# One more step of lead for projections and norms in a hand-scheduled transformer kernel

## The chip, the core and the metric

The kernel runs on one core of a Trainium2 chip. The metric is the device time in microseconds (us) of one execution, and the figure given is the median over runs. TensorE is called PE in the profile, VectorE DVE, ScalarE ACT, GpSimd POOL, SyncE SP. PEld is PE's loading of weights.

## The reference, cut to what matters

The input is 2048 tokens of 128 features. Three modules follow each other: a stack of six local-attention layers, a linear-attention block, and the same stack once more. One layer of the stack is what the change is about:

```python
def attn_layer(x, Wqkv, qs, ksc, Wo):            # 16 heads of 64, windows of 32 tokens
    q, k, v = jnp.split(x @ Wqkv, 3, -1)         # ... split into heads
    q = l2norm(q) * qs
    k = l2norm(k) * ksc
    q = q * cos * scale + rotate_half(q) * sin * scale
    k = k * cos * inv + rotate_half(k) * sin * inv
    out = local_attention(q, k, v)               # each window sees itself and the one before
    return out.transpose(0, 2, 1, 3).reshape(b, n, INNER) @ Wo

def ffn_layer(x, g, bln, W1, b1, W2, b2):
    xn = (x - mu) / jnp.sqrt(var + 1e-05) * g + bln
    a, gate = jnp.split(xn @ W1 + b1, 2, -1)
    return a * jax.nn.gelu(gate, approximate=False) @ W2 + b2

for i in range(DEPTH):                           # DEPTH = 6
    x = attn_layer(shift_tokens(x), ...) + x
    x = ffn_layer(shift_tokens(x), ...) + x
```

The token shift moves half of the features by one token.

## The kernel before

**Tiles and stages.** Features lie on the 128 partitions, tokens along the free axis. A layer is cut into 8 chunks of 256 tokens (`AC`), and the attention of a chunk into 4 steps (`STEPS`): two halves of 128 tokens by two halves of 8 heads. The feed-forward works on blocks of 512 tokens, so one block goes with two chunks, that is with eight steps.

**Order.** Nothing here is left to a planner. The inner function `at(step, pos, fn, ...)` of `ffn_module` (L552) enters a call into a plan under a step and a position in it; at the end the calls are made step by step, in a step by position, inside `manual_schedule` (L599). Each engine carries out its own instructions in that order, and waits where an input or a buffer is not ready. A module has 6 x 8 x 4 = 192 steps, and some more at both ends. `t0` is the first attention step of a chunk.

**The work of one chunk, in the order of its data:**

- `tables` (L187) multiplies the rotation tables by a layer's scales, on POOL, four instructions for q and four for k.
- `project` (L203), four calls g = 0 to 3: eight matmuls p (L218, each instruction of the source runs as two) give a quarter of q and of k in two banks. DVE multiplies each with the tables into `prod` (L224), POOL adds the two halves into `abq` or `abk` (L230), and ACT squares each bank into `sq` (L236). The order of issue is rotation of q, square of k, square of q, rotation of k.
- `square_sums` (L247), two calls: matmuls ss (L254) add the squares up by head into the one bank of `ps_ss`.
- `norms_a` (L310): a maximum on DVE (L314), then Ln, Exp and Square on ACT (L315, L316, L318), which give a first estimate of the inverse norms in `rn`. `norms_b` (L321): two DVE instructions (L325, L326) that refine it.
- `scale_keys` (L342), two calls: four matmul instructions r (L347) spread the norms of the keys over the partitions, into two banks; two DVE multiplies (L353) scale `abk`; then `gather` (L293) issues eight DMAs on SP's queue that lay out the keys in `hk`. Queries are gathered in the same way into `hq`, straight after projection, and their norms go through `query_norms` (L328) into `rq`.
- `values_proj` (L261) and `values_windows` (L276): v by matmul pv (L271), a copy on ACT (L272), and three DMAs on SP into `ve` and `vo`.
- `earlier_keys` (L358): the last window of the chunk before, rotated by matmul pk (L367).
- In the chunk's own steps: `similarities` (L372) with a mask matmul (L383), 32 matmul instructions (L391) and a maximum and a product on DVE (L402, L403, the statistics `st`); `exponentials` (L407), eight on ACT (L417); a step later `normalised` (L424), a reciprocal on DVE and a multiply on POOL; another step later `transposed` (L435), with matmuls te (L443) and copies eT on DVE (L444), and `values` (L446), with matmuls av (L458) and a copy oT on ACT (L464); then `output` (L466), matmuls y (L471) and additions on DVE (L475).
- `feed_forward` (L479) is a generator of which eight pieces are placed at odd steps mostly: mean and squares (`lnsq`), variance, `rstd`, its spreading `rb`, three times a pair of matmuls pf (L513) with a GELU gate on ACT (L518) and a product h on DVE (L522), then yf (L530). Around each gate ACT loads another table set and then the former one (L516, L521).

**Banks.** All matmul results but similarities and square sums come from one pool of five PSUM banks, `small` (L182). A new tile takes the bank that came free longest ago, and PE waits when its readers are not done. `rn` has one buffer, `sq` four, `prod` two, `abq` two and `abk` three.

**Where things stand before.** In numbers of steps modulo 4, with the position in brackets: projection (20) in all steps, its g = 0 in step 1; square sums (45) in steps 2 and 0; `norms_a` (2) and `norms_b` (33) in step 1; `scale_keys` (58) in step 1 and (45) in step 2; values (50) in all steps; gates (57) in steps 3, 1 and 3 of eight.

Of the kernel before, what the change touches and what calls it, by code (L numbers as in the profile page):

```python
# [40 lines left out]
def kernel(ctx: ExitStack, tc: tile.TileContext, a: dict, out: bass.AP):  # L41
# [84 lines left out]
    def ffn_module(m, last):  # L126
        with ExitStack() as st:
# [424 lines left out]
            def at(step, pos, fn, *args):  # L552
                plan.setdefault(step, []).append((pos, len(plan[step]) if step in plan else 0, fn, args))
# [5 lines left out]
            for l in range(DEPTH):  # L559
                for c in range(NAC):  # L560

                    t0 = per * l + STEPS * c
                    if c == 0:
                        at(t0 - 10, 46, tables, l, 0)
                        at(t0 - 8, 46, tables, l, 1)
                    for g in range(4):
                        at(t0 - 7 + g, 20, project, l, c, g)
                        at(t0 - 2 + g, 50, values_proj, l, c, g)
                    for g2 in range(2):
                        at(t0 - 6 + 2 * g2, 45, square_sums, l, c, g2)  # L570
                    for t in range(2):
                        at(t0 - 1 + 2 * t, 62, values_windows, l, c, t)
                    at(t0 - 5, 30, gather, l, c, "q", 0)
                    at(t0 - 3, 1, gather, l, c, "q", 1)
                    at(t0 - 3, 2, norms_a, l, c)
                    at(t0 - 3, 33, norms_b, l, c)
                    at(t0 - 3, 58, scale_keys, l, c, 0)
                    at(t0 - 2, 45, scale_keys, l, c, 1)
                    at(t0 - 2, 46, query_norms, l, c)
                    at(t0 - 1, 45, earlier_keys, l, c)  # L580
                    for s in range(STEPS):
                        at(t0 + s, 25, similarities, l, c, s)
                        at(t0 + s, 30, exponentials, l, c, s, 0)
                        at(t0 + s, 51, exponentials, l, c, s, 1)
                        at(t0 + s + 1, 3, normalised, l, c, s)
                        at(t0 + s + 2, 40, transposed, l, c, s, 0)
                        at(t0 + s + 2, 41, transposed, l, c, s, 1)
                        at(t0 + s + 2, 60, values, l, c, s)
                    for t in range(2):
                        at(t0 + 4 + 2 * t, 55, output, l, c, t)  # L590
                for f in range(NCH):
                    gen = feed_forward(l, f)
                    t0 = per * l + 8 * f
                    for step, pos in (
                        (11, 57), (12, 57), (13, 4), (13, 57),
                        (15, 57), (17, 57), (19, 57), (21, 57),
                    ):
                        at(t0 + step, pos, more, gen)
# [112 lines left out]
    def no_earlier():  # L711

        nc.gpsimd.memset(xa[64:P, 0:1], 0.0)

    ffn_module(0, False)
    linear_module()
    no_earlier()
    ffn_module(1, True)


# [103 lines left out]
```

## Time and profile before

| What | Value |
|---|---|
| Median of 3 runs | 4289.59 us (4288.85 to 4295.82) |
| The profiled execution | 4295.45 us |
| Its span, first to last instruction | 4293.6 us |
| Mean granted TensorE clock | 0.959 |
| PE, PEld | 92%, 64% of the span |
| DVE, ACT, POOL | 63%, 66%, 39% |
| Linear-attention block and norms between the stacks | about 2050 to 2240 us, PE busy 135.84 of 190 us |
| Eight key or query DMAs | some 5 us of SP's queue, 2.1 us to landing for each |

The busy share of an engine is an average over the whole span. A wait is named by the instruction that waits and the one that released it, with the total in us, the number of times and the longest. A line number (L218) is one of the listing above; te, pv, y, av, r, p, pf are the names of PSUM tiles. In a timeline the columns are start, duration, engine, line, operation, tiles written and read, count, and in brackets the idle time before it with its releaser. Busy time of PE is modelled from the starts of its matmuls.

### The profile page before, as it was taken

To read this page: it belongs to the slowest core of one execution; us is meant where nothing else is said; L and a number is where in the kernel's file an instruction comes from. 1 tells how busy PE (TensorE), PEld (TensorE's weight loads), DVE (VectorE), ACT (ScalarE), POOL (GpSimd) and SP (SyncE) were. 2 spreads that over 40 slices of the span, in tenths; PEclk is the share of its full clock that TensorE was granted. 3 is DMA by queue.
4 is the path that set the end of the run, shared out by engine and by line. 5 is a ranking of instruction groups with operands and counts; after the bars stand their busy time and mean duration, and the time that the engine had idled before them with its cause. 6 is when DMAs were issued, how large, how long until landed. Compare 5 with 4: busy or idle time off the path is not lost.

```text
span 4293.6 us, 110203 instructions
## 1 busy us (share of the span) xinstructions
PE 3947.0 (92%) x41968; PEld 2744.5 (64%) x41968; DVE 2719.7 (63%) x5222; ACT 2846.8 (66%) x8784; POOL 1672.7 (39%) x1355
## 2 busy tenths in 40 slices
PE   7899999999999999999777899999999999999998
PEld 4666666666666666666445666666666666666665
DVE  4666666666676666665426566666666666766664
ACT  4676777767667676677225676767667676677766
POOL 4343444344344334332014344343343443443331
PEclk8999999999999999999788999999999999999998
DMA  3343433433334334342003343433434334343331
GB/s 105 86 107 89 101 100 94 103 94 101 97 92 112 93 95 110 87 102 68 8 25 91 85 109 89 104 98 96 101 95 107 93 96 106 87 109 97 91 99 49
DMA packets 323975, 393.67 MB, mean 92 GB/s; under 512 B 61052, under 2 KB 274808, under 8 KB 323448
## 3 DMA queue, kind: packets, MB, share of 16 engines
q1 hardware_dynamic: 323448, 386.61, 35.7%
q8 instruction: 334, 5.47, 0.5%
q14 instruction: 193, 1.58, 0.1%
HBM read 34.58 MB, written 1.05 MB: 8 GB/s over the span
## 4 chain that ended last, share of the span: by engine, by line
PE 23%; ACT 16%; DVE 7%; issue 2%; SPq 1%; DMA 1%; POOL 1%; ACTq 0%; DVEq 0%; POOLq 0%
ACT e L417 8%; PE p L218 5%; DVE prod L224 3%; PE y L471 2%; PE te L443 2%; ACT L516 2%; PE pv L271 2%; PE av L458 2%; PE sim L391 2%; PE ss L254 2%; SPq L305 1%; ACT v L272 1%; DVE sim L402 1%; ACT gate L518 1%; PE yf L530 1%
## 5 line engine op out<-in xcount | busy, mean ns | idle before, releaser
L417 ACT ACTIVATE e<-sim,st,rq 128x96 f32<-128x96 f32 x3072 | 1291.8, 440 | 570.9 <-DVE st L403 509.5
L429 POOL TENSOR_TENSOR e<-e,st 128x768 f32<-128x768 f32 x384 | 564.4, 1470 | 1869.1 <-DVE st L427 1540.3
L224 DVE TENSOR_TENSOR prod<-p,tab 128x1024 f32<-128x1024 f32 x768 | 918.6, 1211 | 235.5 <-ACT sq L236 129.4
L218 PE MATMUL p<-xa,wqk 128*128 128x256 f32 x3072 | 845.0, 420 | 120.4 <-ACT gate L518 115.4
L218 PEld LDWEIGHTS p<-xa,wqk 128*128 128x128 f32 x3072 | 592.0, 204 | 246.6 <-ACT gate L518 138.1
L236 ACT ACTIVATE sq<-p 128x512 f32<-128x512 f32 x768 | 435.6, 599 | 355.6 <-PE p L218 240.0
L417 ACT ACTIVATION_READ_ACCUMULATOR e<-sim,st,rq 128x1 f32 x3072 | 653.9, 213 | 0.0
L230 POOL TENSOR_TENSOR abq<-prod 128x512 f32<-128x512 f32 x384 | 489.0, 1273 | 188.2 <-DVE prod L224 144.4
L230 POOL TENSOR_TENSOR abk<-prod 128x512 f32<-128x512 f32 x384 | 485.7, 1265 | 72.5 <-DVE prod L224 63.7
L444 DVE COPY eT<-te 96x512 f32<-96x512 f32 x768 | 489.8, 677 | 3.6 <-PE te L443 3.6
L522 DVE SCALAR_TENSOR_TENSOR h<-pf,lvec,gate 128x512 f32<-128x512 f32 x144 | 107.9, 749 | 571.1 <-ACT gate L518 553.1
L471 PEld LDWEIGHTS y<-oT,wo 128*128 128x128 f32 x3072 | 374.4, 192 | 95.1 <-issue 49.5
L402 DVE TENSOR_REDUCE sim<-sim 128x4 f32<-128x384 f32 x768 | 426.5, 555 | 9.0 <-PE sim L391 8.8
L443 PE MATMUL te<-sq_consts,e 128*96 128x128 f32 x3072 | 424.1, 279 | 2.5 <-ACT gate L518 0.8
L271 PE MATMUL pv<-wv,xa 128*128 128x512 f32 x768 | 415.4, 623 | 10.6 <-DVE rstd L499 8.4
L458 PE MATMUL av<-eT,ve 96*64 96x64 f32 x6144 | 406.9, 229 | 4.6 <-DVE eT L444 4.5
L458 PEld LDWEIGHTS av<-eT,ve 96*64 96x64 f32 x6144 | 318.3, 138 | 132.5 <-issue 50.5
L272 ACT COPY v<-pv 128x512 f32<-128x512 f32 x384 | 227.6, 593 | 255.3 <-DMA ve<-v 171.1
L458 PE MATMUL av<-eT,vo 96*64 96x64 f32 x6144 | 385.8, 223 | 0.0
L471 PE MATMUL y<-oT,wo 128*128 128x128 f32 x3072 | 376.4, 276 | 4.5 <-ACT gate L518 3.0
L391 PEld LDWEIGHTS sim<-hk,hq 64*64 64x64 f32 x12288 | 279.1, 136 | 151.7 <-issue 136.4
L443 PEld LDWEIGHTS te<-sq_consts,e 128*96 128x96 f32 x3072 | 317.6, 127 | 59.5 <-DVE h L522 11.8
(141 smaller groups left out, 4954.9 us busy)
## 6 DMA issues: line engine op xcount, KB each, us to landing
hq<-abq SPq DMA_DIRECT2D x1536, 64.0 KB, 2.1
hk<-abk SPq DMA_DIRECT2D x1536, 64.0 KB, 2.1
vo<-v SPq DMA_DIRECT2D x192, 384.0 KB, 4.3
ve<-v SPq DMA_DIRECT2D x192, 256.0 KB, 3.5
ve<-v SPq DMA_DIRECT2D x180, 128.0 KB, 2.3
wqk<-in_Wqk SPq DMA_DIRECT2D x48, 256.0 KB, 3.6
wv<-in_Wv SPq DMA_DIRECT2D x24, 256.0 KB, 2.8
wo<-in_Wo SPq DMA_DIRECT2D x12, 512.0 KB, 5.0
```

What stands on the lines that cost most here:

```text
L218: nc.tensor.matmul(both[s][:, u, :], wqk[g][:, 2 * s + u, :], xs, start=True, stop=True)
L224: nc.vector.tensor_tensor(prod, both[s].unsqueeze(2).to_broadcast([P, 2, 2, AC]), tabs[l, s].rearrange("p (u v) t -> p u v t", u=2), ALU.mult,
L230: nc.gpsimd.tensor_tensor(d["qk"[s], g // 2][:, :, g % 2, :], prod[:, 0], prod[:, 1], ALU.add)
L236: nc.scalar.activation(sq, both[s], AF.Square)
L271: nc.tensor.matmul(ps, xa[:, ti * P : (ti + 1) * P], wv[j], start=True, stop=True)
L402: nc.vector.tensor_reduce(peaks[par], sims[par], AX.X, ALU.max, negate=True)
L417: nc.scalar.activation(e[:, par, i, :], d["sims", step][par][:, i, :], AF.Exp, bias=st8[:, 0, par, i : i + 1], scale=rq[:, par, i : i + 1] ...
L429: nc.gpsimd.tensor_tensor(ef, ef, st8[:, 1].rearrange("p r i -> p (r i)").unsqueeze(2).to_broadcast([P, 8, SK]), ALU.mult,)
L443: nc.tensor.transpose(te3[0:SK, i, :], d["e", step][:, par, i, :], ident)
L444: nc.vector.tensor_copy(d["eT", step][:, 4 * par : 4 * par + 4, :], te3[0:SK])
L458: nc.tensor.matmul(av3[64 * par : 64 * par + 64, i, SQ * s : SQ * s + SQ], d["vs", t][s][:, h * DH : (h + 1) * DH], d["eT", step][:, 4 * p ...
L471: nc.tensor.matmul(y[:, 0:P], wo[:, i, :], d["oT", t][:, i, :], start=(i == 0), stop=(i == 7))
```

## The change

Only the plan's numbers change. Each call does what it did.

- `tables` and `project` run one step earlier; so do `square_sums`, which also go from position 45 to 61, behind the products with v.
- `norms_a`, `norms_b` and the second gather of queries run one step earlier, at the positions that they had.
- `scale_keys` stay in their steps and go from positions 58 and 45 to 27, directly behind the similarities (25) and ahead of the first exponentials (30).

```diff
                     if c == 0:
-                        at(t0 - 10, 46, tables, l, 0)
-                        at(t0 - 8, 46, tables, l, 1)
+                        at(t0 - 11, 46, tables, l, 0)
+                        at(t0 - 9, 46, tables, l, 1)
                     for g in range(4):
-                        at(t0 - 7 + g, 20, project, l, c, g)
+                        at(t0 - 8 + g, 20, project, l, c, g)
                         at(t0 - 2 + g, 50, values_proj, l, c, g)
                     for g2 in range(2):
-                        at(t0 - 6 + 2 * g2, 45, square_sums, l, c, g2)
+                        at(t0 - 7 + 2 * g2, 61, square_sums, l, c, g2)
                     for t in range(2):
                         at(t0 - 1 + 2 * t, 62, values_windows, l, c, t)
                     at(t0 - 5, 30, gather, l, c, "q", 0)
-                    at(t0 - 3, 1, gather, l, c, "q", 1)
-                    at(t0 - 3, 2, norms_a, l, c)
-                    at(t0 - 3, 33, norms_b, l, c)
-                    at(t0 - 3, 58, scale_keys, l, c, 0)
-                    at(t0 - 2, 45, scale_keys, l, c, 1)
+                    at(t0 - 4, 1, gather, l, c, "q", 1)
+                    at(t0 - 4, 2, norms_a, l, c)
+                    at(t0 - 4, 33, norms_b, l, c)
+                    at(t0 - 3, 27, scale_keys, l, c, 0)
+                    at(t0 - 2, 27, scale_keys, l, c, 1)
                     at(t0 - 2, 46, query_norms, l, c)
```

After it the square sums stand in steps 1 and 3 modulo 4, the norms in step 0, and projection g = 0 in step 0.

## The prediction, on record before the result

> **What bounds the kernel now.** I read the page first (busy shares), then TensorE's waits, then the timelines of PE, ACT and DVE over one cycle of eight steps, then the granted clock in small windows.
>
> ```profile
> PE 3947.0 (92%) x41968; PEld 2744.5 (64%) x41968; DVE 2719.7 (63%) x5222; ACT 2846.8 (66%) x8784; POOL 1672.7 (39%) x1355
> ```
>
> PE is nearly always busy, so an edit pays only through PE's gaps. Its waits (total us, times, longest):
>
> ```profile
> PE p L218 <- ACT gate L518: 115.4, 84, 1.9
> PE ss L254 <- ACT sq L236: 54.9, 50, 4.2
> PE r L347 <- DVE rn L326: 33.9, 10, 5.5
> ```
>
> The schedule repeats every eight steps (two chunks, one feed-forward block); I number a step by its index modulo 8. Starts of the projection matmuls (p) give one clean cycle, 601.27 to 683.19 us, 81.92 us: steps 4, 5, 6, 7, 0, 1, 2, 3 last 11.20, 10.12, 10.18, 8.20, 10.69, 10.70, 11.80 and 9.03. The first wait in the list has two members per cycle, 0.87 us in step 4 and 1.88 us at the start of step 2 (44 x 1.88 + 40 x 0.87 = 117.5, against 115.4). The square sums wait 0.91 us in step 0; r waits 0.30 in step 1. Together 3.96 us of stall. The 1.88 us one has a second cost:
>
> ```profile
> 660.45:662.36 1.91, 0.03 (x3) 1.00 0.00 0
> 662.36:665.70 3.34, 3.34 (x10) 0.60 0.03 8
> ```
>
> Columns: stretch, length, PE busy, granted clock. Behind the stall the clock falls to 0.60 here (0.50 elsewhere) and eight p matmuls take 3.16 us, not 1.99; with mask and similarities this cycle lost 1.67 us. From 2715.20 to 4117.43 us there are 17 cycles of 82.48 us on average, so the mean loss is 1.67 + 0.56 = 2.2 us.
>
> The steps with a GELU gate are 7, 1 and 3. Here ACT after step 3's exponentials, then DVE and PE in step 4 (which starts at 601.27):
>
> ```profile
> 601.23 1.28 ACT L516 ACT_TABLE_LOAD   x1
> 602.53 0.68 ACT L518 ACTIVATE gate<-pf,lvec 85x512 f32<-85x512 f32 x1
> 603.23 1.28 ACT L521 ACT_TABLE_LOAD   x1
> 604.62 0.63 ACT L89 ACTIVATE lnsq<-xc 128x512 f32<-128x512 f32 x1
> 605.16 0.57 ACT L464 COPY oT<-av 128x512 f32<-128x512 f32 x1
> 605.62 1.09 ACT L236 ACTIVATE sq<-p 128x512 f32<-128x512 f32 x2
> ```
> ```profile
> 606.32 1.22 DVE L224 TENSOR_TENSOR prod<-p,tab 128x1024 f32<-128x1024 f32 x1 [0.54 <-ACT sq L236]
> ...
> 608.80 1.27 DVE L444 COPY eT<-te 96x512 f32<-96x512 f32 x2
> ```
> ```profile
> 603.27 1.13 PE L218 MATMUL p<-xa,wqk 128*128 128x256 f32 x4 [0.87 <-ACT gate L518]
> ...
> 606.48 1.34 PE L254 MATMUL ss<-sq,sel 128*32 128x256 f32 x16
> ...
> 611.38 0.33 PE L458 MATMUL av<-eT,ve 96*64 96x64 f32 x4
> ```
>
> The reader is to see a chain: gate and its two table loads hold ACT until 604.5, the squares start 4.35 us into step 4 (2.03 in a step without gate before it), the second rotation waits for a square, the eT copies end 8.8 us in, and PE reaches the products with v (av) only at 10.1. PE's own work is just long enough to hide the gate.
>
> [...] the trace shows DVE's rotation waiting 0.54 us for ACT's square of the same bank. [...]
>
> **The change, part by part.**
>
> *Spread of key norms (scale_keys) to position 27.* The 1.88 us exists because step 1 hands out banks in the order pf, pf, r, r, av, and with five banks, passed on in the order in which they come free, the next p takes the one that the gate reads. With r ahead of the transposes, p takes the banks of te and pv, free long before; the gate's two go to r, 3.1 us into step 2, when gate and h are over. Gone: 1.88 us, the 0.30, and the clock loss behind it. What is late next: the tile 5 allocations behind r. r's readers are two DVE multiplies (0.60 us apart) that start after the reductions, 5.2 us into a step, so r's banks come free at 5.9 and 6.5. In step 2 pv takes the first; PE is there at 1.83 + 0.42 + 0.82 + 0.63 + 0.95 + 0.55 = 5.2 (p, mask, similarities, r, te, nt). Stall 0.7 in step 6, and 1.2 in step 2, where the gate makes DVE some 0.4 late. In steps 1 and 5 pf and yf take it: PE at 5.45, stalls 0.5 and 0.6. Sum 3.0 us of new stall. eT copies are 1.25 us later (7.7), av comes at 7.8 or later: hidden. The price could lie below nothing only if DVE ran ahead of today's rows; upper end 4.5.
>
> *Square sums to position 61.* ss (1.00 to 1.28 us) moves from even to odd steps. Its 0.91 us wait goes, and so does its place in front of av. Steps 3 and 7, 1 and 5 get 1.0 us longer; 4, 0, 2 and 6 shorter by 1.28, 1.61, 1.0 and 1.0. In step 4 the 0.87 us goes too: ss now lies between the gate's matmuls and p.
>
> *Norms one step earlier: the costly part.* norms_a (ACT Ln, Exp, Square: 652.53 to 653.69 in the timeline, 1.16 us; DVE maximum 0.43) and norms_b (DVE, 0.79) were in steps 1 and 5, behind a step with no gate. Now they are in steps 0 and 4, always right behind a gate of step 7 or 3, in the chain above and ahead of squares and eT copies. Step 4: squares 13.38 us after step 3's start become 14.54; second rotation 15.24; statistics 17.7; norms_b 18.5; eT 19.8. PE starts step 4 at 9.03 + 1.0 and is at av 8.0 later, 18.05. Step 4 then ends at 19.8 + 1.09 = 20.9 after step 3's start (20.23 now). Step 0, without lnsq: squares 13.99 after step 7's start, eT 19.25, PE at av 16.05, end 20.35 (18.89 now). PE's idle time there is 3.2 us in step 0 (about 1 of it ahead of y, whose bank waits for a square) and 2.0 in step 4.
>
> *Projections and tables one step earlier.* The same matmuls, rotations (1.21 us), POOL adds (1.27) and 8 table multiplies of POOL per layer (0.92), at the same place in a step: nothing, hidden as now; the feed-forward that they read ends 2.4 steps earlier. One more prologue step against a lighter end, per module: -5 to +8 us, taken as 0. Projection buffers: abk is rewritten sooner. The key gather (8 DMAs, 5.1 to 6.1 us of SP's queue, landing 2.1 us after the last) now starts at 6.5 in steps 1 and 5, ends about 4.5 us into the next step, and POOL wants the buffer at 4.0: up to 0.6 us of POOL, which is 39% busy: nothing. On SP the gather passes ahead of the v windows (3 x 0.63 us); they issue about 2.5 us into the even step, land 2.3 later, and the v copy that today waits for them (171.1 us of ACT in all) is due at 6.6: hidden, and better than now. SP's sum per chunk is 4 x 6.1 + 6 x 0.63 = 28 of some 41 us.
>
> **Sum of a cycle.** Step 3: 10.0; 4: 10.85; 5: 10.12 + 1.05 + 0.6 = 11.8; 6: 10.18 - 1.0 + 0.7 = 9.9; 7: 9.2; 0: 11.15; 1: 10.70 - 0.30 - 1.88 + 1.0 + 0.5 = 10.0; 2: 11.80 - 1.67 - 1.0 + 1.2 = 10.3. Together 83.2 us, against 82.48 with clock loss. Stalls: 5.2 + 3.0 = 8.2 where 3.96 went. The clock is the unknown: stalls of 1 and 2.2 us close together in step 0 resemble the 1.88 that costs 2.2; they could cost 0 to 3. Half of today's loss, 1.1, makes 84.3, or +1.8 us a cycle. By the count above 44 cycles are complete: +79 us on 4289.6, so 4369. The profiled execution took 4295.45 us (span 4293.6), 5.9 above the median of the runs; the sum is a difference and goes onto the median.
>
> **Rivals.**
> - *Full clock loss* behind the stalls of steps 0 and 4 (2.2 to 3): 83.2 + 2.6 = 85.8, +3.3 x 44: 4435. For it: nearly every 1.88 us stall has it. Against: PE's idle time is now in two pieces. Chance 0.17.
> - *Banks don't bind* (DVE's multiplies earlier than I put them, or other banks free): 3.0 us a cycle less, 84.3 - 3.0 = 81.3, -1.2 x 44: 4237, faster. For it: today's list shows DVE seldom holding PE. Chance 0.14.
> - *The norms find room*, ending on the other side: one mechanism, the chain from the gate to eT in steps 0 and 4. If squares and rotation do not slip by the 1.16 us, or PE is later at av than I say, its 5.2 us of stall go: 84.3 - 5.2 = 79.1, -3.4 x 44: 4140. It decides from about 1.8 us: if av waits less than 3.4 us per cycle instead of 5.2, the kernel is faster. Against it: ACT runs in order and gate, loads and copies are fixed in length. Chance 0.12.
> - *Nothing changes*, the removed 1.88 and the new av stalls just cancel: 4290. Chance 0.07.
>
> **Numbers.** The forecast has 0.50, its own range 4316 (no clock loss) to 4410. Slower by over 0.2%, which is about what a measurement of this kernel can tell from no change: 0.50 + 0.17 = 0.67; faster 0.26; same 0.07. The range 4215 to 4445 leaves out the norms' rival (0.12) and a tail above.
>
> **What would show it.** Right: the wait p <- gate nearly gone; a new wait av <- eT in TensorE's list near 44 x 4 = 180 us, in steps 0 and 4; pv, pf and yf waiting for abk L353, 100 to 130 us; y waiting for a square; ACT's v no longer waiting for ve; squares starting 4.5 us and more into steps 0 and 4. Wrong: av's wait under 80 us in all, or p still waiting for the gate.

## The result, and the profile after

The changed kernel took 4424.78 us (median) beside 4292.7 for the kernel before in the same runs: ratio 1.031, interval 1.0284 to 1.0335, slower. The forecast was 4369 us with a range of 4215 to 4445. The loss is 132 us where 79 were forecast. The profiled execution has a span of 4424.0 us.

The page after, TensorE's busy line:

```profile
PE 3938.7 (89%) x41968; PEld 2737.0 (62%) x41968; DVE 2760.9 (62%) x5222; ACT 2846.1 (64%) x8784; POOL 1678.9 (38%) x1355
```

PE is busy 8.3 us less than before in a span 130.4 us longer: the loss is idle time, not slower work. The mean clock is even higher, 0.965 against 0.959. TensorE's waits after (total us, times, longest):

```profile
PE av L458 <- DVE eT L444: 97.6, 117, 1.9
PE pv L271 <- DVE abk L353: 97.2, 94, 1.4
PE y L471 <- ACT sq L236: 56.0, 90, 1.1
PE av L458 <- ACT v L272: 44.9, 44, 1.0
PE yf L530 <- DVE abk L353: 39.7, 42, 1.5
PE pf L513 <- DVE abk L353: 25.8, 41, 1.0
...
PE ss L254 <- ACT sq L236: 14.1, 8, 4.2
```

The three waits that led the list before are gone or small (r's wait for `rn`, 33.9 us before, is down to 4.2). Two families stand in their place. One is behind the norms: av and y, 97.6 + 44.9 + 56.0 = 198.5 us (the 44.9 belong here: this wait stands in step 4 and is gone in the kernel with the norms put back, below). The other is the wait for a bank that the keys' multiplies read: 97.2 + 39.7 + 25.8 = 162.7 us. ACT's wait for `ve` is down from 171.1 us to 1.3.

Here are ACT, DVE and PE in one step 0, which starts at 3032.20 us. ACT first (start, duration, engine, line, operation):

```profile
3032.12 1.28 ACT L516 ACT_TABLE_LOAD   x1
3033.42 0.69 ACT L518 ACTIVATE gate<-pf,lvec 128x512 f32<-128x512 f32 x1
3034.12 1.28 ACT L521 ACT_TABLE_LOAD   x1
3035.41 0.59 ACT L464 COPY oT<-av 128x512 f32<-128x512 f32 x1
3035.90 0.38 ACT L315 ACTIVATE ss<-ss 128x256 f32<-128x256 f32 x1
3036.31 0.37 ACT L316 ACTIVATE ss<-ss 128x256 f32<-128x256 f32 x1
3036.71 0.38 ACT L318 ACTIVATE rn<-ss 128x256 f32<-128x256 f32 x1
3036.99 1.08 ACT L236 ACTIVATE sq<-p 128x512 f32<-128x512 f32 x2
```
```profile
3037.68 1.23 DVE L224 TENSOR_TENSOR prod<-p,tab 128x1024 f32<-128x1024 f32 x1 [1.27 <-ACT sq L236]
...
3040.16 0.41 DVE L325 SCALAR_TENSOR_TENSOR rn<-rn,ss 128x256 f32<-128x256 f32 x1
3040.61 0.42 DVE L326 SCALAR_TENSOR_TENSOR rn<-rn,ss 128x256 f32<-128x256 f32 x1
3040.95 1.28 DVE L444 COPY eT<-te 96x512 f32<-96x512 f32 x2
```
```profile
3032.20 1.99 PE L218 MATMUL p<-xa,wqk 128*128 128x256 f32 x8
...
3038.13 2.05 PE L471 MATMUL y<-oT,wo 128*128 128x128 f32 x16 [0.92 <-ACT sq L236]
...
3041.68 0.33 PE L458 MATMUL av<-eT,ve 96*64 96x64 f32 x2 [1.50 <-DVE eT L444]
...
3042.28 0.27 PE L458 MATMUL av<-eT,ve 96*64 96x64 f32 x1 [0.27 <-DVE eT L444]
...
3043.51 3.46 PE L218 MATMUL p<-xa,wqk 128*128 128x256 f32 x8
```

It is the predicted chain: gate and loads until 3035.40, oT, the norms' three operations, and only then the squares, 4.8 us into the step. The second rotation waits 1.27 us for a square, `norms_b` sits ahead of the eT copies, and PE loses 0.92 us ahead of y and 1.77 ahead of av. Behind them the next eight p take 3.46 us where those at the start of this step took 1.99. In windows of PE (stretch, length, busy time of PE, PEld, DVE, ACT and POOL, granted clock, DMA share, GB/s) the clock is 0.54 there:

```profile
3037.00:3043.40 6.40, 3.71 (x49) 3.17 (x48) 4.93 (x11) 4.78 (x20) 2.45 (x2) 0.98 0.22 53
3043.40:3046.80 3.40, 3.40 (x10) 2.62 (x9) 1.31 (x2) 0.78 (x3) 1.47 (x1) 0.54 0.00 0
```

Step lengths in us, from the starts of p between 2700 and 3500 us; "usual" is the most frequent value of the 9 or 10 repeats:

| Step | 0 | 1 | 2 | 3 | 4 | 5 | 6 | 7 | sum |
|---|---|---|---|---|---|---|---|---|---|
| predicted, without clock loss | 11.15 | 10.0 | 10.3 | 10.0 | 10.85 | 11.8 | 9.9 | 9.2 | 83.2 |
| after, usual (step 1: shortest) | 10.99 | 10.27 | 10.33 | 10.03 | 10.75 | 12.68 | 10.20 | 9.17 | 84.4 |
| after, mean | 11.27 | 11.00 | 10.37 | 10.06 | 10.75 | 12.91 | 10.20 | 9.08 | 85.6 |
| before, mean | 10.73 | 10.69 | 11.83 | 9.15 | 11.20 | 10.12 | 10.18 | 8.65 | 82.6 |

### The profile page after: what moved, and what is told of

It reads as the page before. It is cut to its first block, busy times and chain, and to the rows that moved or that the text cites. A ratio compares the mean times of both kernels' runs of the same rounds, so it can differ in the third digit from the quotient of the medians.

```text
span 4424.0 us, 110387 instructions
## 1 busy us (share of the span) xinstructions
PE 3938.7 (89%) x41968; PEld 2737.0 (62%) x41968; DVE 2760.9 (62%) x5222; ACT 2846.1 (64%) x8784; POOL 1678.9 (38%) x1355
## 4 chain that ended last, share of the span: by engine, by line
PE 18%; ACT 14%; DVE 11%; issue 3%; DMA 3%; SPq 2%; POOL 1%; DVEq 0%; ACTq 0%; POOLq 0%
ACT e L417 6%; PE p L218 5%; DVE prod L224 4%; PE av L458 3%; DVE sim L402 2%; PE y L471 2%; ACT sq L236 2%; ACT L516 2%; PE pv L271 1%; DVE abk L353 1%; SPq L305 1%; PE yf L530 1%; DMA ve<-v 1%; ACT L521 1%; ACT v L272 1%
## 5 line engine op out<-in xcount | busy, mean ns | idle before, releaser
L224 DVE TENSOR_TENSOR prod<-p,tab 128x1024 f32<-128x1024 f32 x768 | 932.2, 1218 | 538.5 <-PE p L218 300.3
L218 PE MATMUL p<-xa,wqk 128*128 128x256 f32 x3072 | 820.6, 413 | 4.7 <-issue 2.5
L236 ACT ACTIVATE sq<-p 128x512 f32<-128x512 f32 x768 | 423.4, 598 | 477.8 <-PE p L218 424.7
L458 PE MATMUL av<-eT,ve 96*64 96x64 f32 x6144 | 444.3, 232 | 142.6 <-DVE eT L444 97.6
L230 POOL TENSOR_TENSOR abk<-prod 128x512 f32<-128x512 f32 x384 | 485.5, 1264 | 162.7 <-DVE prod L224 140.0
L458 PEld LDWEIGHTS av<-eT,ve 96*64 96x64 f32 x6144 | 351.9, 141 | 299.6 <-DVE eT L444 133.6
L271 PE MATMUL pv<-wv,xa 128*128 128x512 f32 x768 | 414.5, 622 | 97.3 <-DVE abk L353 97.2
L471 PE MATMUL y<-oT,wo 128*128 128x128 f32 x3072 | 392.0, 282 | 60.5 <-ACT sq L236 56.0
L458 PE MATMUL av<-eT,vo 96*64 96x64 f32 x6144 | 411.3, 227 | 0.0
L464 ACT COPY oT<-av 128x512 f32<-128x512 f32 x384 | 226.1, 589 | 193.2 <-PE av L458 191.9
```

Of the source, the lines that this page charges most:

```text
L218: nc.tensor.matmul(both[s][:, u, :], wqk[g][:, 2 * s + u, :], xs, start=True, stop=True)
L224: nc.vector.tensor_tensor(prod, both[s].unsqueeze(2).to_broadcast([P, 2, 2, AC]), tabs[l, s].rearrange("p (u v) t -> p u v t", u=2), ALU.mult,
L230: nc.gpsimd.tensor_tensor(d["qk"[s], g // 2][:, :, g % 2, :], prod[:, 0], prod[:, 1], ALU.add)
L236: nc.scalar.activation(sq, both[s], AF.Square)
L271: nc.tensor.matmul(ps, xa[:, ti * P : (ti + 1) * P], wv[j], start=True, stop=True)
L458: nc.tensor.matmul(av3[64 * par : 64 * par + 64, i, SQ * s : SQ * s + SQ], d["vs", t][s][:, h * DH : (h + 1) * DH], d["eT", step][:, 4 * p ...
```

## The experiments

Each experiment was timed beside runs of the kernel before, and experiments are compared by that ratio, with its 95% interval in brackets; 1% is some 43 us. Means of steps are of the 8 to 10 repeats between 2700 and 3500 us of the profiled execution. In the diffs, + is the experiment.

**Theory and rivals.** The theory is the prediction's: norms behind a gate hold eT and so av (steps 0 and 4), and the early spread makes PE wait for a bank. The rivals: the lead as such costs nothing and the early spread is the loss; or the loss is a matter of place only, and another place for the norms takes it away.

### The norms at the end of their step

```diff
-                    at(t0 - 4, 2, norms_a, l, c)
-                    at(t0 - 4, 33, norms_b, l, c)
+                    at(t0 - 4, 52, norms_a, l, c)
+                    at(t0 - 4, 56, norms_b, l, c)
```

> The changed kernel with one edit: norms_a goes from position 2 to 52 and norms_b from 33 to 56 of the same step, behind the exponentials. Chain theory (the norms stand behind the gate, ahead of squares and eT copies, in steps 0 and 4): squares start about 1.2 us earlier in these steps, eT ends 2 us earlier, so av waits 1.2 us in step 0 and not at all in step 4, and the clock loss behind it goes for the most part: 4.0 + 1.5 us per cycle of 44, about 4425 - 240 = 4185 us, faster than before (4293). Rival, spread theory (the loss comes from banks held by the key spread): av's waits are only a symptom, PE waits for abk instead, 4400 or more. pv, pf and yf should wait for abk as now (163 us) under both.

Measured: 4422.09 us, ratio 1.0296 (1.0278 to 1.0313), no gain where 240 us were expected. On average step 0 did shorten, from 11.27 us to 9.16, and step 4 from 10.75 to 8.92. The time came back one step on: step 1 went from 11.00 to 11.68 us and step 5 from 12.91 to 16.08. DVE's waits and two of TensorE's in this kernel:

```profile
DVE rn L325 <- ACT rn L318: 260.4, 96, 6.8
```
```profile
PE te L443 <- ACT sq L236: 71.2, 88, 1.4
PE te L443 <- DVE rstd L499: 58.6, 44, 2.7
```

`norms_b` stands at the end of the step on DVE and waits for `norms_a` on ACT, which comes after all exponentials. What is queued behind it on DVE is the next step's rotation; its banks come free later, and now te waits for one. So removing the stall of steps 0 and 4 is possible, and the place chosen only moved it.

### The same, with the spread at the head of the step

On top of the last diff:

```diff
-                    at(t0 - 3, 27, scale_keys, l, c, 0)
-                    at(t0 - 2, 27, scale_keys, l, c, 1)
+                    at(t0 - 3, 19, scale_keys, l, c, 0)
+                    at(t0 - 2, 19, scale_keys, l, c, 1)
```

> The changed kernel with the norms at positions 52 and 56 as in the first run, and scale_keys at position 19, ahead of the projections, in the same steps. The multiplies of the key spread then fall into DVE's idle time at a step's start, and r's banks come free early: pv, pf, yf no longer wait for abk (-3.6 us per cycle), while p waits about 0.6 to 1.2 us for the gate in step 2 (+0.9). From 4185: -2.7 x 44 = 4065 us (4030 to 4120). If the bank waits are only moved into DVE's lateness, no better than the first run.

Measured: 4571.0 us, ratio 1.0642 (1.0626 to 1.0658), a clear miss (4065 was expected). TensorE's first wait:

```profile
PE r L347 <- DVE st L427: 318.4, 94, 9.3
```

r is the first instruction of the step on PE here and needs `rn` from a DVE that is still held by the late `norms_b`: in a timeline `norms_b` ends at 3063.91 us, `st`, which the list names, is the next on DVE, and r starts at 3064.05, after 3.10 us of waiting. The spread can't stand ahead of everything when the norms end the step before.

### The early spread alone, in the kernel before

```diff
-                    at(t0 - 3, 33, norms_b, l, c)
-                    at(t0 - 3, 58, scale_keys, l, c, 0)
-                    at(t0 - 2, 45, scale_keys, l, c, 1)
+                    at(t0 - 3, 26, norms_b, l, c)
+                    at(t0 - 3, 27, scale_keys, l, c, 0)
+                    at(t0 - 2, 27, scale_keys, l, c, 1)
```

> The kernel before with only the key spread moved to position 27 (norms_b at 26, so that it stands ahead of it). The 1.88 us of p behind the gate, 0.30 of r and most of the 2.2 us clock loss per cycle go (-4.4); norms_b and the two multiplies now stand ahead of what pf and yf wait for in steps 1 and 5 (+1.3 and +2.5). Chain theory: -0.6 us per cycle, 4265 us (4220 to 4310), so the spread alone does not make the loss. Spread theory: 4340 or more.

Measured: 4626.78 us, ratio 1.0769 (1.0753 to 1.0785), another miss. By the number alone the rival was right (4340 or more), but the wait is not the rival's wait for a bank; it is the last run's, in purer form:

```profile
PE r L347 <- DVE rn L326: 372.7, 96, 9.7
```

Norms and spread are in the same step; r waits 2.99 us in step 1 and 4.32 in step 5 on average, with te, pv and all that follows queued behind it on PE. So the early spread needs the norms' lead, and the two parts of the change can be separated in one direction only: from after, by putting the spread back.

### The spread put back, and the lead alone

```diff
-                    at(t0 - 3, 27, scale_keys, l, c, 0)
-                    at(t0 - 2, 27, scale_keys, l, c, 1)
+                    at(t0 - 3, 58, scale_keys, l, c, 0)
+                    at(t0 - 2, 45, scale_keys, l, c, 1)
```

> The changed kernel with scale_keys back at positions 58 and 45. The 163 us of pv, pf and yf behind abk go; p behind the gate in step 2 comes back, but with 1.0 us of square sums in between, so some 0.9 us x 44 = 40 us. pv in step 2 then takes a bank of te and waits for the late eT copy, 1 to 2.5 us per cycle. Chain theory: the av waits of steps 0 and 4 stay near 140 us, in all 4360 (4300 to 4420), still slower than before. Spread theory: the whole loss goes, 4290 or less.

Measured: 4369.54 us, ratio 1.0175 (1.0159 to 1.019). Its waits:

```profile
PE av L458 <- DVE eT L444: 93.0, 116, 1.9
PE pv L271 <- DVE eT L444: 72.7, 94, 1.1
PE y L471 <- ACT sq L236: 56.0, 90, 1.1
PE p L218 <- ACT gate L518: 50.9, 42, 1.3
```

All waits for `abk` are gone. av and y stay as they were: they don't depend on the spread. Even so PE waits for a bank, pv for one of te's that DVE has still to copy.

With the square sums at 45 on top of that, so that only the one step of lead is left of the change:

```diff
-                        at(t0 - 7 + 2 * g2, 61, square_sums, l, c, g2)
+                        at(t0 - 7 + 2 * g2, 45, square_sums, l, c, g2)
```

> The kernel before with only the lead of one step (tables, projections, sums, norms, second gather of queries), all positions as before: square sums at 45, scale_keys at 58 and 45. Chain theory: step 0 and 4 have their long chain, so most of the loss is here: 4369 as measured without the early spread, plus 0.28 us for each of four square sums per cycle in the dearer place, 4395 us (4350 to 4430). Rival, that the lead is free and the positions make the loss: 4293.

Measured: 4409.67 us, ratio 1.0269 (1.0251 to 1.0287), as expected: the lead alone makes most of the loss, and the sums behind the products with v, the only difference from the kernel with the spread put back, take back 0.94 points of it, 40 us.

### The square sums put back under the full change

> The kernel after with the sums of squares alone put back from 61 to 45, ahead of the products with v. If moving them is worth under the full change what it was worth on top of the lead alone (40 us): about 4465 us. Rival (the early spread has taken over what the sums were in the way of): within 10 us of the kernel after, 4415 to 4435.

The diff is the last one, with the spread left at 27. Measured: 4449.76 us, ratio 1.0344 (1.0329 to 1.036), between the two expectations: 0.34 points, some 15 us, on the ratios. This interval and that of the kernel after (1.0284 to 1.0335) overlap, so it is not shown that moving the sums helps here; what is shown is that it is worth less than the 40 us that it was worth without the early spread.

### The norms' arithmetic taken out

These two kernels leave the normalisation of q and k out.

```diff
-                nc.scalar.activation(ss[:, 1, :], ss[:, 0, :], AF.Ln)
-                nc.scalar.activation(ss[:, 1, :], ss[:, 1, :], AF.Exp, scale=-0.5)
-                nc.scalar.activation(rn, ss[:, 1, :], AF.Square)
+                nc.scalar.activation(rn, ss[:, 0, :], AF.Exp, scale=-(2.0**-60))
...
-                nc.vector.scalar_tensor_tensor(rn, rn, -0.5, ss[:, 0, :], ALU.mult, ALU.mult)
-                nc.vector.scalar_tensor_tensor(rn, rn, 1.5, ss[:, 1, :], ALU.add, ALU.mult)
```

In the kernel after:

> The changed kernel with the norms' arithmetic cut out: of norms_a the maximum and one ACT function are left (an Exp that gives about 1), norms_b is empty, so keys and queries are not normalised. The chain in steps 0 and 4 becomes 0.8 us (two ACT functions) plus 0.79 us (two DVE instructions) shorter. Chain theory: waits of y and av fall by about 1.6 us in step 0 and 1.6 in step 4, and half of the clock loss goes: -3.1 - 1.0 per cycle, 4245 us (4200 to 4320). Rival, spread theory: the work lies beside PE's, 4400 or more.

In the kernel before:

> The same cut of the norms' arithmetic in the kernel before, where the norms stand in steps 1 and 5, behind a step without a gate. Chain theory: there they are hidden, av comes late enough and p waits for the gate all the same: 4285 us, at most 0.5% less than before (4270 to 4297). If the cut alone made a kernel faster by some per cent, the run before this one would say nothing of the chain.

Measured: 4275.18 us (0.9973, interval 0.9955 to 0.9992) and 4231.24 (0.9859, interval 0.9835 to 0.9884). The cut is worth 3.37 points in after and 1.41 in before. The second was expected at 0.5 at most. Where it comes from can be read by comparing the starts of ACT's copies oT, one per step, in the profiled executions. Of the 68 us that the cut gains in the kernel before, 47 lie ahead of the thirteenth copy of each of the two modules. There stand r's ten waits for `rn`, the 33.9 us of the prediction's list, and they are gone with the cut. Over all the other steps the gain is 20 us, 0.5 us per cycle, which is what was expected. In after, the same count gives 34 of 157 us at the starts of the modules and 124 in the other steps, 2.8 us per cycle. There y's wait for a square is gone and av's for eT is down to 61.5 us from 97.6, while the waits for `abk` stay (96.9, 48.2 and 27.1 us). So in the regular cycles the arithmetic costs 2.3 us more in its new place, some 100 us; one ACT operation and the maximum were still there.

### The feed-forward moved away from step 0

```diff
-                        (11, 57), (12, 57), (13, 4), (13, 57),
-                        (15, 57), (17, 57), (19, 57), (21, 57),
+                        (13, 57), (14, 57), (15, 4), (15, 57),
+                        (17, 57), (19, 57), (21, 57), (23, 57),
```

In the kernel after the gates then stand in steps 1, 3 and 5, so that step 0 follows none:

> The changed kernel with the eight pieces of a feed-forward block two steps later, so that gates stand in steps 1, 3 and 5 of eight instead of 7, 1 and 3. Step 0, where norms stand, then follows a step with no gate; step 4 still follows one. Chain theory: the waits of y and av in step 0 (0.9 and 2.2 us) go, those in step 4 rise to about 3 us since the variances no longer lie in it, clock loss behind one of two: about -2 us per cycle net, 4425 - 90 = 4335 us (4280 to 4380). Rival, that the order of the norms against the gates doesn't matter and the loss comes from the key spread alone: 4425 within 0.5%.

Measured: 4306.88 us, ratio 1.0034 (1.0024 to 1.0044). Step 0, with the same instructions on PE as before the edit, is down from 11.27 to 8.40 us on average, y doesn't wait there and av 0.27 us, and step 1 behind it is down from 11.00 to 10.31. That is 3.56 us per cycle, where the cycle as a whole became 3.3 us shorter (85.6 to 82.4): the other six steps, among which the feed-forward's work moved, add up to nearly the same. Step 4, which still follows a gate but has lost the variances, now has the stalls that step 0 had: 0.76 (y) and 1.78 us (av), where it had 0.43 and 1.02. So the loss at step 0 is the gate ahead of the norms, its clock loss in step 1 with it. Part of the gain is clock: the whole trace has 247 us at half clock beside 315 in after (mean clock 0.972 beside 0.965), which is at most 34 of the 118 us.

The same edit in the kernel before is the control:

> The kernel before with the feed-forward's pieces two steps later (gates in steps 1, 3 and 5), the same edit that took 118 us off the kernel after; a control. Chain theory: that gain came from what step 0 no longer does behind a gate, so here, where the norms follow no gate in either order, nothing of it comes back; instead two gates now end in steps that hand out banks as step 1 does, two long waits of p for the gate in a cycle in place of one long and one of 0.9 us, with their clock loss, against the 0.9 us of the square sums in step 0: 1.0 + 1.1 us a cycle on 82.5, about 4385 us (4300 to 4430). Rival (the feed-forward simply stands better two steps later, whatever the norms do): about 118 us less than before, 4175.

Measured: 4401.91 us, ratio 1.0248 (1.0219 to 1.0277). The feed-forward doesn't stand better there by itself. TensorE's first waits:

```profile
PE av L458 <- ACT gate L518: 79.9, 42, 1.9
PE p L218 <- ACT gate L518: 79.0, 42, 1.9
```

Two waits of 1.9 us per cycle, as expected, though the second falls on av and not on p; in that step the feed-forward's mean takes a bank too, which would shift the order by one. The gain of the last kernel thus depends on what the change had put into step 0.

### Norms and spread put back, the rest of the lead kept

```diff
-                    at(t0 - 4, 2, norms_a, l, c)
-                    at(t0 - 4, 33, norms_b, l, c)
-                    at(t0 - 3, 27, scale_keys, l, c, 0)
-                    at(t0 - 2, 27, scale_keys, l, c, 1)
+                    at(t0 - 3, 2, norms_a, l, c)
+                    at(t0 - 3, 33, norms_b, l, c)
+                    at(t0 - 3, 58, scale_keys, l, c, 0)
+                    at(t0 - 2, 45, scale_keys, l, c, 1)
```

> The kernel after with the norms and the spread of the keys put back where they were (norms one step later again at 2 and 33, spread at 58 and 45): tables, projections, squares' sums (still behind the products with v) and the second gather keep their lead. Chain theory (the loss sits where step 0's and 4's norms follow a gate on ACT and hold eT): it goes with the norms' lead; the gate's wait at p returns at about 0.9 us, v's products with a bank of te 0.7 to 1 us per chunk; 79.5 to 80 us a cycle, about 4185 us (4140 to 4240), faster than before. Rival (the lead of the projections or the place of the sums costs by itself): 4293 or more.

Measured: 4270.46 us, ratio 0.9931 (0.9916 to 0.9946): faster than before, by 30 us and not by 108. Of the norms' lead this is the direct test: between this kernel and the one with the spread put back lies nothing else, and they differ by 2.44 points, some 105 us. Steps 0 and 4 are 9.20 and 8.94 us (11.03 and 10.92 there). The clock has no part in it: 284 and 274 us at half clock in the two traces (mean clock 0.967 and 0.969). By the starts of the copies oT the later norms win 125 us in the regular steps, 2.8 us per cycle, and lose 29 at the starts of the modules, where r's waits for `rn` are back (39.5 us in all).

With the last section this makes a cross. In step 0, with the same instructions on PE, norms behind a gate take 11.27 us (after; 11.03 with the spread put back), norms without the gate 8.40, and the gate without norms 9.20. Only the two together make the step over 11 us long. The waits of the kernel of this section, and its PE in one step 2:

```profile
PE pv L271 <- DVE eT L444: 72.9, 94, 1.1
PE av L458 <- DVE eT L444: 44.0, 96, 0.7
...
PE p L218 <- ACT gate L518: 37.0, 42, 0.9
...
PE yf L530 <- ACT sq L236: 23.2, 42, 0.9
```
```profile
3034.54 1.99 PE L218 MATMUL p<-xa,wqk 128*128 128x256 f32 x8 [0.88 <-ACT gate L518]
...
3040.78 1.65 PE L271 MATMUL pv<-wv,xa 128*128 128x512 f32 x2 [0.92 <-DVE eT L444]
3042.22 3.11 PE L471 MATMUL y<-oT,wo 128*128 128x128 f32 x16
```

The miss has places. In step 2, pv waits 0.92 us, and then pv and y run slowly (y 3.11 us, 1.95 in step 4): the step is 11.8 us long in 8 of 10 repeats and 10.17 in the other two, so it loses 1.65 us that I had not counted. In step 1 r waits 0.76, in step 5 yf 0.53 us.

One position changed on top, so that r no longer takes a bank ahead of pv in step 2:

```diff
-                    at(t0 - 2, 45, scale_keys, l, c, 1)
+                    at(t0 - 2, 52, scale_keys, l, c, 1)
```

> The last kernel with the second half of the keys' spread at 52 in place of 45, so that it no longer takes its banks among the similarities of eT. Chain theory: the wait of v's products for a bank goes, 1.6 us a cycle less than the last kernel: about 4115 us (4080 to 4200). Rival (the bank's wait only moves to another taker): within 0.5% of the last kernel.

Measured: 4251.98 us, ratio 0.9889 (0.9873 to 0.9906), the fastest kernel here with the whole computation. pv's wait for eT is out of the list, and step 2 takes 9.93 us in nine of ten repeats (10.02 in the other), with p's wait of 0.88 still in it. But step 3 went from 10.13 to 10.94 us on average: there a mask matmul now waits in some repeats for ACT's exponentials (`sim <- e`, 31.7 us in 35 waits; 17.8 in 19 ahead of the edit) and pf for a bank of te; these waits are 0.5 of the 0.8 us. The chain theory's wait went, but the size, 0.42 points, is the rival's (within 0.5%): half of what step 2 gained was given back one step later.

## Why the prediction was right, and what was off

**Sign and order of size** came out of the predicted mechanism; the loss is 1.7 times the forecast. Point by point:

- *The wait of p for the gate gone.* Right; it isn't in the list after. The 0.30 us of r went too. What the prediction has in its list and left out of its count are r's ten waits for `rn`, 33.9 us, all at the starts of the modules; they fell to 4.2.
- *New waits for the banks of r.* Predicted 3.0 us per cycle, measured 162.7 / 44 = 3.7: pv 2.2 (1.9 predicted), pf 0.6 (0.5), yf 0.9 (0.6). After against the kernel with the spread put back, the early spread costs 1.35 points, 58 us. As a part it was valued wrongly: by the prediction's terms (1.88, 0.30 and 1.67 us of clock gone, 3.0 new) it gains 0.85 us per cycle. But with the sums behind the products with v, the wait of p that it removes is 50.9 / 44 = 1.2 us and not 1.88. The sum of the whole change doesn't depend on this.
- *Square sums.* Right: their wait fell from 54.9 to 14.1 us, steps 3 and 7 are 10.03 and 9.17 us (10.0 and 9.2 predicted).
- *Norms behind a gate.* Right in place and nearly in size: 198.5 / 44 = 4.5 us per cycle for 5.2 predicted. In the cycles of the table it is 2.6 in step 0 (3.2 predicted) and 1.45 in step 4 (2.0); the rest of the 198.5 lies mostly at the starts of the modules. Shown twice: by putting back the norms (105 us), and by taking the gate away from step 0 (3.56 us in steps 0 and 1, nearly all that the cycle gained).
- *Projections and tables at no cost.* Not measured alone. Together with the sums' new place and the second gather they gain 30 us. The sums' place was worth 40 us where it was measured without the early spread, so a cost of some 10 us, or more, could hide in them. One more step at the start of a module was put at 0: after's thirteenth copy oT comes 4 and 6 us later in the two modules. v's copy hardly waits for `ve` any more, as predicted.
- *Clock.* The allowance was 1.1 us per cycle. Mean less usual lengths is 85.6 - 84.4 = 1.2 us, most of it in step 1 (0.7). The trace's record of the granted clock agrees: in these 800 us it has eight stretches at half clock, six from the end of step 0 on and two in step 5, 27.3 us in all beside 37.5 in before.

**The term that was mis-sized** is step 5: 11.8 predicted, 12.68 measured, 0.88 of the 1.2 us by which the sum without clock loss was short. The others are step 1 (+0.27), step 6 (+0.30), steps 0 and 4 (-0.26). 1.2 x 44 = 53 us, and 4369 + 53 = 4422. That this meets 4424.78 so closely is partly luck: over all steps behind the thirteenth of each module the loss is 2.7 us per cycle in the profiled executions, and 3.0 in the stretch of the table. DVE and PE in step 5, which starts at 3086.37 us, and PE in step 5 of before, which starts at 2995.83:

```profile
3087.65 0.16 DVE L495 SCALAR_TENSOR_TENSOR rstd<-var,rstd 128x4 f32<-128x4 f32 x1 [0.81 <-ACT rstd L494]
3087.84 0.66 DVE L498 TENSOR_SCALAR rstd<-rstd 128x4 f32<-128x4 f32 x1
3088.54 0.16 DVE L499 TENSOR_TENSOR rstd<-rstd,var 128x4 f32<-128x4 f32 x1
3088.62 2.36 DVE L224 TENSOR_TENSOR prod<-p,tab 128x1024 f32<-128x1024 f32 x2
...
3092.55 1.29 DVE L353 TENSOR_TENSOR abk<-abk,r 128x512 f32<-128x512 f32 x2 [0.24 <-issue]
```
```profile
3091.03 1.13 PE L271 MATMUL pv<-wv,xa 128*128 128x512 f32 x2
3093.30 2.84 PE L530 MATMUL yf<-h,w 128*128 128x512 f32 x6 [1.14 <-DVE abk L353]
```
```profile
2999.82 1.02 PE L271 MATMUL pv<-wv,xa 128*128 128x512 f32 x2
3000.68 2.74 PE L530 MATMUL yf<-h,w 128*128 128x512 f32 x6
```

I took the multiplies to start 5.2 us into every step. In step 5 the feed-forward's `rstd` comes first on DVE, the rotations start 2.25 us into the step (1.24 in step 6) and the multiplies at 6.18 (5.53 in step 6). So yf's stall is 1.14 us here and 1.03 on average, and not 0.6. From start to start it weighs more: yf follows 2.27 us behind pv where it followed 0.86 behind it before, 1.41 us in place of 0.6. This is nearly the whole 0.88. The `rstd` instructions are in the profile of before too; I had read the start from other steps. Some 0.5 us of it could not be read there: L498 takes 0.66 us in all nine repeats after and 0.17 in all ten before. POOL's multiply of the same time, in the timeline of POOL:

```profile
3087.01 1.47 POOL L429 TENSOR_TENSOR e<-e,st 128x768 f32<-128x768 f32 x1 [3.75 <-DVE st L427]
```

It ends at 3088.48, and L498 at 3088.50. Of the 48 L498 in this trace the 44 that start while POOL's multiply runs take 0.66 us and end 0.02 to 0.03 behind it; the other four take 0.17. In before 46 of 48 take 0.17; the two that start while the multiply runs take 0.61 and 0.66. In the kernel with the norms at the end of their step one takes 1.44 us:

```profile
3085.36 1.44 DVE L498 TENSOR_SCALAR rstd<-rstd 128x4 f32<-128x4 f32 x1
```

Not every DVE instruction took longer there: L495 ran beside the same multiply in all 44 cases and took its 0.16 us. Why L498 does and L495 does not is not shown.

**The rivals.** Full clock loss (2.6 us) did not come, banks did bind, and norms found no room. That last rival was sized wrongly too: without the norms' stall I had put the kernel at 4140 us, and when the stall was taken away by experiment, with the spread back in its old place too, other waits and the clock left 4270.

**What stays open.** A place for the norms that keeps their lead without either stall was not found. Their lead kept for the first chunks of a module alone, where it is worth 29 us, was not tried. The lead of projections and tables was not measured without the sums' new place.

## What to carry to other kernels

More lead was no slack here, where it moved the norms behind a gate on ACT, which did its work in the order of the plan (step 0 took 11.27 us with both, 8.40 and 9.20 with one of the two): look at what stands ahead of it and behind it in the new step, on each engine it uses. With five banks that go round in turn, moving an allocation exchanged one wait for another (115.4 us of p for the gate before, 162.7 us of pv, yf and pf for the keys' multiplies after); find the instruction that will take each bank next, and when its last reader ends in that very step, not in a typical one. Undo the parts of a change one at a time from the changed side: some can't be done alone from the other.

## What was not expected of the hardware

- Two waits of 0.88 and 0.92 us some 5 us apart were followed by slow matmuls in 8 of 10 cycles. Windows of the kernel with norms and spread put back (columns as above) show a clock of 0.63 behind the second:

```profile
3034.60:3040.70 6.10, 5.27 (x58) 3.91 (x58) 6.03 (x12) 4.09 (x9) 2.70 (x2) 1.00 0.17 42
3040.70:3045.30 4.60, 4.52 (x20) 3.58 (x20) 1.92 (x5) 1.08 (x5) 1.07 (x1) 0.63 0.59 135
```

  With the second wait taken away (spread at 52), the first alone left step 2 at 9.93 us in nine of ten repeats. The granted clock there is 1.00 from 3025.40 us, where p starts behind its wait, to 3035.30, and between 2700 and 3500 us no group of eight p takes over 2.14 us and no pair of pv over 1.13.
- The half clock came in blocks. In the clock records of before and after each of the 68 and 69 stretches at half clock starts within 0.01 us of one grid of 3.41 us and lasts a whole number of its intervals; only the last one of a trace, at its end, has another length. In after 51 of 69 last one interval, in before 38 of 68.
- Whether a stall was followed by a block went with where it fell on that grid. I take the stalls between 300 and 2000 and between 2500 and 4250 us. In before, 34 of the 40 waits of p of 1.88 us were followed by half clock; these began in the first 2.53 us of an interval, the other six later than 2.6. In after, 20 of the 39 waits of av of 1.5 us were followed by it; these began between 3.24 us of an interval and 1.35 us of the next, the other 19 between 1.37 and 2.82. So a stall of one size cost clock or not by the phase of the schedule; why is not shown.
- A DVE instruction of 128x4 elements (L498) took 0.66 us instead of 0.17 in the 44 of 48 cases of after in which it started during a POOL multiply of 1.47 us (shown above). Moving work changed such meetings as well: before had two of them.
